# Context tiles of a cross-attention kernel: transposes moved from TensorE to VectorE blocks and DMAs inside SBUF

## The chip, the core and the metric

The kernel runs on one core of a Trainium2 chip. The metric is device time in microseconds (us). The kernel before takes 2022.62 us, the median of three runs from 2022.18 to 2022.88.

## The reference

`x` is 4096 x 512 and the context `ctx_1024` is 3202 x 512, all float32. What matters is the first half:

```
xn, cn = layernorm(x, g1, beta1), layernorm(ctx, g1, beta1)
q, k, v = heads(xn @ Wq.T + bq), heads(cn @ Wk.T + bk), heads(cn @ Wv.T + bv)   # 8 heads of 64
x1 = x + softmax(q k^T / 8) v @ W_o.T + b_o
U  = (layernorm(x1, g2, beta2) @ W_in.T + b_in) @ Bmat
s_t = silu(s_{t-1} @ A.T) + u_t          # a scan over 4096 steps
out = x1 + s @ Cmat + (mean(ctxb) @ W_prog.T + b_prog)
```

The change touches only the normalised context: how its transpose, with the 512 features on partitions, is made before the products that give `k` and `v`.

## The kernel before, in words

The program has a first stage, here called the preparation, and then the attention proper, whose instructions are put in order by a planner (`Plan`) that works with costs and due times; the scan follows interleaved with it. The change lies wholly in the preparation, whose order is written out by hand: inside `tc.manual_schedule()` every engine runs its instructions in the order of the source.

The preparation walks over 26 chunks of 128 context rows (the last has 2) in the loop `for c in range(NCH)`, line 545. Four chunks form a group (`GC = 4`). For chunk c the source order is:

1. `load_chunk(c + 7)`: SP issues the load of a raw chunk into `cx`, one of eight buffers (L509).
2. `norm_chunk(c + 3)`: VectorE takes the statistics (L245, L247), POOL makes two factors (L254 to L258), ScalarE writes the normalised chunk `xh` (L266), one of three buffers.
3. TensorE makes `pv`, eight matmuls of 128 x 512 against `wv` (L555).
4. `turn_chunk(c + 2)`: TensorE transposes `xh` in four 128 x 128 pieces into PSUM (`tp_c`, L282), and ScalarE (even chunks) or VectorE (odd chunks) copies the result into `ct` (L523). `ct` holds the turned chunks of one group, and there are two such buffers.
5. ScalarE copies `pv` to `vs`, one of three buffers (L568), and SP stores it to HBM as `vd` (L569).
6. One piece of side work (`work`, `first`): gains, biases, other small products and the loads of other weights, which ScalarE's queue issues: `raw_q`, `win`, `bm`, `bi`, `cb`, `rowb`, `modb`, `wp_t`, `a_t`, `wo`, `x0`.

After the fourth chunk of a group TensorE makes four `pk`, each eight matmuls against `wk` (L588). ScalarE writes each to `ks`, one of three buffers (L596), and SP stores each with two DMAs to `kd` (L601). PSUM has two buffers for `pv` and two for `pk`.

Two things about queues matter. SP and ScalarE each issue their DMAs in program order, and an instruction that waits holds up all that stands behind it on its engine. And the program has eight semaphores for the completion of these DMAs, `DMAHW0` to `DMAHW7`, which SP's and ScalarE's DMAs take in turn: a DMA is issued only when the one that had its semaphore before has landed.

Of the kernel before, what the change touches and what calls it, by code (L numbers as in the profile page):

```python
# [10 lines left out]
F32 = mybir.dt.float32  # L11
# [7 lines left out]

T, S2, H, NH, HD, NS = 4096, 3202, 512, 8, 64, 64  # L20
P = 128
NC = H // P
NCH = 26
CK = 128
NDC = NCH // 2
REST = S2 - (NCH - 1) * CK
GC = 4
QB = 512
NQB = T // QB
NT = QB // P  # L30
QU = QB // 2
# [20 lines left out]
def keys(c):  # L52


    return CK if c < NCH - 1 else REST
# [7 lines left out]
def key0(c):  # L63
    return c * CK
# [105 lines left out]
def xattn_ssm_kernel(  # L170
# [22 lines left out]
    nc = tc.nc  # L193
# [3 lines left out]

    kd = dram.tile([NC, NDC, P, 2 * CK], F32, name="kd")
    vd = dram.tile([NC, NDC, CK, 2, P], F32, name="vd")
    const = ctx.enter_context(tc.tile_pool(name="const", bufs=1))  # L200

    u = const.tile([P, L, NCK], F32, name="u")
    END = NCK - QU // L
    nc.gpsimd.memset(u[NS:, :, END:], 0.0)

    ident = const.tile([P, P], F32, name="ident")
    make_identity(nc, ident)
# [3 lines left out]
    nc.vector.tensor_tensor(twice, ident[:, :HD], ident[:, HD:], ALU.add)  # L211
    shifts = const.tile([P, NQB * NC], F32, name="shifts")
    kx = const.tile([P, NC, HD], F32, name="kx")
    vx = const.tile([P, H], F32, name="vx")
    nc.gpsimd.memset(vx, 0.0)
    neg_half = const.tile([P, 1], F32, name="neg_half")
    nc.gpsimd.memset(neg_half, -0.5)
    g1s = const.tile([P, NC], F32, name="g1s")
    be1s = const.tile([P, NC], F32, name="be1s")
    g2s = const.tile([P, NC], F32, name="g2s")  # L220
# [20 lines left out]
    def stats(xt, n, name, pool=None):  # L241

        pool = pool or ln
        st = pool.tile([P, nc.vector.BN_STATS_DIM], F32, tag="st", name=f"st_{name}")
        nc.vector.bn_stats(st[:n], xt[:n])  # L245
        mv = pool.tile([P, nc.vector.BN_AGGR_DIM], F32, tag="mv", name=f"mv_{name}")
        nc.vector.bn_aggr(mv[:n], st[:n])  # L247
        return mv

    def factors(mv, n, name, pool=None):  # L250

        pool = pool or ln
        ve = pool.tile([P, 1], F32, tag="ve", name=f"ve_{name}")
        nc.gpsimd.tensor_scalar(ve[:n], mv[:n, 1:2], EPS, None, ALU.add)  # L254
        rstd = pool.tile([P, 1], F32, tag="rstd", name=f"rstd_{name}")
        nc.gpsimd.tensor_tensor(rstd[:n], ve[:n], neg_half[:n], ALU.pow)
        nmr = pool.tile([P, 1], F32, tag="nmr", name=f"nmr_{name}")
        nc.gpsimd.tensor_scalar(  # L258
            nmr[:n], mv[:n, 0:1], rstd[:n], -1.0, ALU.mult, ALU.mult
        )  # L260
        return rstd, nmr
# [9 lines left out]
    def normalize(xt, n, name, later=False, pool=None):  # L271

        fs = factors(stats(xt, n, name, pool), n, name, pool)
        last = partial(scaled, xt, fs, n, name, pool)
        return last if later else last()

    def transposes(pool, tag, xh, n, name):

        name = f"tp_{name}"
        tp = pool.tile([P, NC, P], F32, tag=tag, name=name) if pool else m_tile([P, NC, P], name)  # L280
        for c in range(NC):
            nc.tensor.transpose(  # L282
                tp[:, c, :n], xh[:n, c * P : (c + 1) * P], ident[:n, :n]
            )
        return tp[:, :, :n]

    xp_ = actx.enter_context(tc.tile_pool(name="xp", bufs=2))
    xnp = actx.enter_context(tc.tile_pool(name="xnp", bufs=2))
    qp = actx.enter_context(tc.tile_pool(name="qp", bufs=6))
# [68 lines left out]
    cin = prep.enter_context(tc.tile_pool(name="cin", bufs=3))  # L358
    ctp = prep.enter_context(tc.tile_pool(name="cT", bufs=2))
# [6 lines left out]
    def fetch_w(k, queue, part=slice(0, NC)):  # L366
        queue.dma_start(raw[k][:, part], wsrc[:, part, k * H : (k + 1) * H])
# [135 lines left out]
    cxs, xhs, cts = {}, {}, {}  # L503
# [7 lines left out]

    def norm_chunk(c):
        if c < NCH:
            xhs[c] = normalize(cxs.pop(c), keys(c), f"c{c}", pool=cin)

    def turn_chunk(c):
        if c < NCH:
            g, n = c // GC, keys(c)
            if c % GC == 0:
                cts[g] = ctp.tile([P, NC, GC * CK], F32, tag="ct", name=f"ct_{g}")  # L520
            o = key0(c) - key0(g * GC)
            copy = nc.vector.tensor_copy if c % 2 else nc.scalar.copy
            copy(cts[g][:, :, o : o + n], transposes(kps, "t", xhs.pop(c), n, f"c{c}"))  # L523

    with tc.manual_schedule():
        load_chunk(0)
        nc.scalar.dma_start(g1s, g1)
        fetch_w(2, nc.scalar, slice(0, NC // 2))
        fetch_w(2, nc.sync, slice(NC // 2, NC))
        load_chunk(1)  # L530
        load_chunk(2)
        fetch_w(1, nc.scalar)
        load_chunk(3)
        for t, src in ((be1s, beta1), (bqkv, b_qkv), (g2s, g2), (be2s, beta2)):
            nc.sync.dma_start(t, src)
        for c in range(4, 7):
            load_chunk(c)
        norm_chunk(0)
        gain(2, wv)
        turn_chunk(0)  # L540
        norm_chunk(1)
        norm_chunk(2)
        work = side()
        first = shift(1)
        for c in range(NCH):
            load_chunk(c + 7)
            norm_chunk(c + 3)
            g, n = c // GC, keys(c)
            ct, o = cts[g], key0(c) - key0(g * GC)
            pv = kps.tile([P, 512], F32, tag="v", name=f"pv_{c}")  # L550
            parts = 1 if c < NCH - 1 else 2
            for i in range(NC // parts):
                for h in range(parts):
                    k = h * NC // parts + i
                    nc.tensor.matmul(  # L555
                        pv[h * HD : h * HD + n, :H],
                        ct[:, k, o : o + n],
                        wv[:, k, :],
                        start=(i == 0),
                        stop=(i == NC // parts - 1),  # L560
                        skip_group_check=True,
                    )
            if c == 0:
                turn_chunk(1)
            turn_chunk(c + 2)
            if c < NCH - 1:
                vs = cin.tile([CK, NC, P], F32, tag="vs", name=f"vs_{c}")
                nc.scalar.copy(vs, pv)  # L568
                nc.sync.dma_start(vd[:, c // 2, :, c % 2, :].rearrange("h p d -> p h d"), vs)  # L569
            else:  # L570
                second = wp.tile([n, H], F32, name="second")
                nc.scalar.copy(second, pv[HD : HD + n])
                nc.vector.tensor_tensor(vx[:n], pv[:n], second, ALU.add)
                nc.sync.dma_start(vx[HD : HD + n], vx[:n])
            if c < GC:
                if c == 1:
                    gain(1, wk)
                for _ in range((0, 1, 1, 1)[c]):
                    next(first)
            else:  # L580
                next(work, None)
            if c % GC < GC - 1 and c < NCH - 1:
                continue
            n_g = o + n
            for hp in range(NC):
                pk = kps.tile([P, 512], F32, tag="k", name=f"pk_{g}_{hp}")
                for i in range(NC):
                    nc.tensor.matmul(  # L588
                        pk[:, :n_g],
                        wk[:, i, hp * P : (hp + 1) * P],  # L590
                        ct[:, i, :n_g],
                        start=(i == 0),
                        stop=(i == NC - 1),
                    )
                ks = cin.tile([P, GC * CK], F32, tag="ks", name=f"ks_{g}_{hp}")
                nc.scalar.activation(  # L596
                    ks[:, :n_g], pk[:, :n_g], AF.Identity, bias=bias[:, NC + hp : NC + hp + 1]
                )
                for b in range(g * GC, c + 1, 2):
                    m, k = blocks(b // 2) * CK, key0(b) - key0(g * GC)  # L600
                    nc.sync.dma_start(kd[hp, b // 2, :, :m], ks[:, k : k + m])  # L601
                if g == 0:
                    nc.gpsimd.tensor_copy(kx[:, hp, REST:], ks[:, : HD - REST])
                elif c == NCH - 1:
                    nc.gpsimd.tensor_copy(kx[:, hp, :REST], ks[:, CK : CK + REST])
                for _ in range(2 if g > 1 else 1):
                    next(work, None)
        left = sum(1 for _ in work)
        assert left == 0, left
# [1074 lines left out]
    with tc.manual_schedule():  # L1684
        for g in range(AHEAD_K):
            load_k(*steps[g])
        for g in range(AHEAD):
# [4 lines left out]
                xn=2, xh=2, max=2, rd=2, o_=12,  # L1692
# [25 lines left out]
    n = nc.values_load(nbad[0:1, 0:1], min_val=0, max_val=P * (NCK + P // LT + 3 * len(units)))  # L1718
# [88 lines left out]
```

## Time and profile before

| what | before |
|---|---|
| median of the runs | 2022.62 us |
| the profiled execution's own time | 2022.73 us |
| its span, first to last instruction | 2020.9 us |
| PE (TensorE) busy | 1983.2 us, 98% |
| VectorE busy | 1170.6 us, 58% |
| ScalarE busy | 1160.3 us, 57% |
| POOL busy | 789.3 us, 39% |
| granted TensorE clock, mean | 0.995 |
| end of the preparation's last `pk` on PE | 215.1 us into the span |
| PE busy from 45 to 215 us | 169.8 of 170 us |
| VectorE busy from 45 to 215 us | 35.4 of 170 us |
| ScalarE busy from 45 to 215 us | 52.4 of 170 us |
| share of the 16 DMA engines from 45 to 215 us | 0.38 |

PE is the engine that does the matmuls, PEld its weight loads, which lie beside matmuls. Times within the span count from its first instruction. "Busy" leaves out the issuing of DMAs, so SP has no busy time in the page; its DMA instructions are seen in the timeline, in rows marked SPq. In a timeline a row gives its start, its length, the engine, the line, the operation, the tile written and the tiles read, and how many instructions were merged in it.

### The profile page before, as it was taken

Reading aid. Unit: us, or ns where it says so; the run is one execution under the profiler, and the core shown is the slowest. Engines: PE = TensorE matmul, PEld = TensorE weight load, DVE = VectorE, ACT = ScalarE, POOL = GpSimd, SP = SyncE. Lnnn points to the kernel's source line nnn. Section 1 sums busy time; section 2 is a strip of 40 time slices with the busy share of each in tenths; the row PEclk is TensorE's granted clock in tenths of the full one; section 3 lists DMA queues with packets and bytes.
Section 4 is the critical chain, followed back from the end, with each engine's and each line's share of the span. In section 5 each row is a group of like instructions: output and inputs, shape, how many; then the busy total and the mean of one; then the engine's idle time right before and its main releaser. Section 6 shows DMA issues by size and latency. Waiting matters only on the chain.

```text
span 2020.9 us, 66912 instructions
## 1 busy us (share of the span) xinstructions
PE 1983.2 (98%) x29534; PEld 1324.9 (66%) x29534; DVE 1170.6 (58%) x1481; ACT 1160.3 (57%) x1530; POOL 789.3 (39%) x631
## 2 busy tenths in 40 slices
PE   8999999999999999999999999999999999999996
PEld 4445676776677667766677667766776667766764
DVE  4321366566665666566656666566656665666575
ACT  2233566566665566556656666556655665665653
POOL 2111244235533453245523553345324552345424
PEclk9999999999999999999999999999999999999998
DMA  5632322122222322122222222232212322444475
GB/s 169 192 99 68 99 79 83 54 80 90 88 67 78 97 79 67 55 62 93 81 59 80 90 88 67 78 96 79 67 55 62 93 81 59 144 136 129 130 208 192
DMA packets 187030, 190.66 MB, mean 94 GB/s; under 512 B 20904, under 2 KB 160168, under 8 KB 186732
## 3 DMA queue, kind: packets, MB, share of 16 engines
q1 hardware_dynamic: 182184, 178.62, 29.4%
q10 hardware_dynamic: 4548, 7.67, 1.2%
q8 instruction: 235, 3.85, 0.8%
q14 instruction: 63, 0.52, 0.1%
HBM read 156.32 MB, written 29.88 MB: 92 GB/s over the span
## 4 chain that ended last, share of the span: by engine, by line
PE 78%; DVE 10%; POOL 7%; issue 3%; ACT 1%; DMA 1%; DVEq 0%; POOLq 0%; ACTq 0%
PE po L749 27%; PE s L639 27%; DVE acc L717 6%; PE pq L312 5%; PE pk L588 4%; PE pv L555 4%; POOL acc L717 4%; PE pa L933 4%; PE pd L767 1%; DVE rd L802 1%; ACT p L709 1%; PE tp_x L282 1%; DVE acc L703 1%; POOL acc L724 1%; PE sm L657 1%
## 5 line engine op out<-in xcount | busy, mean ns | idle before, releaser
L709 ACT ACTIVATE p<-s,shifts 128x1024 f32<-128x1024 f32 (+1 forms) x832 | 894.1, 1081 | 522.8 <-PE s L639 510.4
L717 DVE TENSOR_TENSOR acc<-p,acc 128x1024 f32<-128x1024 f32 (+1 forms) x515 | 620.0, 1204 | 406.9 <-POOL acc L717 310.6
L639 PE MATMUL s<-q,k 64*64 64x256 f32 x12800 | 841.4, 378 | 2.7 <-ACT p L709 1.1
L749 PE MATMUL po<-p,v 64*64 64x256 f32 x12800 | 823.2, 376 | 0.0
L717 POOL TENSOR_TENSOR acc<-p,acc 128x1024 f32<-128x1024 f32 x189 | 446.9, 2365 | 809.1 <-DVE acc L717 484.1
L639 PEld LDWEIGHTS s<-q,k 64*64 64x64 f32 x12800 | 483.9, 133 | 217.2 <-issue 21.4
L749 PEld LDWEIGHTS po<-p,v 64*64 64x64 f32 x12800 | 489.5, 133 | 189.0 <-issue 2.2
L724 POOL TENSOR_TENSOR acc<-acc 128x512 f32<-128x512 f32 x64 | 104.5, 1633 | 135.8 <-DVE acc L717 118.0
L717 DVE TENSOR_TENSOR acc<-p,p 128x1024 f32<-128x1024 f32 x64 | 84.6, 1322 | 60.1 <-ACT p L709 54.1
L312 PE MATMUL pq<-xn,wq 128*128 128x256 f32 x512 | 119.0, 385 | 0.0
L802 DVE RECIPROCAL rd<-rd 128x256 f32<-128x256 f32 (+1 forms) x65 | 112.4, 1729 | 2.2
L312 PEld LDWEIGHTS pq<-xn,wq 128*128 128x128 f32 x512 | 94.6, 190 | 23.2 <-issue 11.6
L933 PE MATMUL pa<-wo,o 128*128 128x512 f32 x240 | 107.0, 599 | 0.0
L782 DVE TENSOR_TENSOR o<-po,o 128x256 f32<-128x256 f32 x64 | 27.2, 424 | 128.4 <-ACT o L778 128.2
L555 PE MATMUL pv<-wv,ct 128*128 128x512 f32 (+1 forms) x208 | 96.4, 616 | 1.0 <-ACT ct L523 0.7
L588 PE MATMUL pk<-ct,wk 128*128 128x512 f32 (+1 forms) x224 | 88.8, 549 | 0.0
L321 ACT ACTIVATE q<-pq,bias 128x512 f32<-128x512 f32 x32 | 22.0, 687 | 108.6 <-PE pq L312 108.6
L933 PEld LDWEIGHTS pa<-wo,o 128*128 128x128 f32 x240 | 44.4, 190 | 56.0 <-issue 55.8
L703 DVE TENSOR_TENSOR acc<-x,acc 2x256 f32<-2x256 f32 x128 | 78.1, 610 | 3.0
L523 DVE COPY ct<-tp_c 128x512 f32<-128x512 f32 (+1 forms) x13 | 8.5, 651 | 105.9 <-PE tp_c L282 105.9
L555 PEld LDWEIGHTS pv<-wv,ct 128*128 128x128 f32 (+1 forms) x208 | 38.3, 193 | 44.5 <-issue 41.7
L588 PEld LDWEIGHTS pk<-ct,wk 128*128 128x128 f32 x224 | 39.2, 190 | 42.6 <-issue 42.6
(213 smaller groups left out, 1224.1 us busy)
## 6 DMA issues: line engine op xcount, KB each, us to landing
k<-kd SPq DMA_DIRECT2D x432, 128.0 KB, 2.2
v<-vd SPq DMA_DIRECT2D x432, 128.0 KB, 2.2
xr<-in_x_dram SPq DMA_DIRECT2D x32, 256.0 KB, 4.5
x1d<-xr SPq DMA_DIRECT2D x32, 256.0 KB, 2.2
x<-in_x_dram SPq DMA_DIRECT2D x28, 256.0 KB, 3.2
cx<-in_ctx_dram SPq DMA_DIRECT2D x25, 256.0 KB, 3.0
vd<-vs SPq DMA_DIRECT2D x25, 256.0 KB, 2.4
kd<-ks SPq DMA_DIRECT2D x48, 128.0 KB, 1.8
```

Of the source, the lines that this page charges most:

```text
L312: nc.tensor.matmul(pq[:, half * QU : (half + 1) * QU], wq[:, i, hp * P : (hp + 1) * P], xns[half][:, i, :], start=(i == 0), stop=(i == NC ...
L555: nc.tensor.matmul(pv[h * HD : h * HD + n, :H], ct[:, k, o : o + n], wv[:, k, :], start=(i == 0), stop=(i == NC // parts - 1), skip_group_ ...
L588: nc.tensor.matmul(pk[:, :n_g], wk[:, i, hp * P : (hp + 1) * P], ct[:, i, :n_g], start=(i == 0), stop=(i == NC - 1),)
L639: nc.tensor.matmul(s[k0 : k0 + HD, a, b, :], kts[(*w["at"][:2], c)][r, b * CK + k0 : b * CK + k0 + HD], q[r], start=True, stop=True, skip_ ...
L703: nc.vector.tensor_tensor(to[r], t[r], to[r], ALU.add)
L709: nc.scalar.activation(t[:, :, :nb, :], w["ps"][c][:, :, :nb, :], AF.Exp, bias=w["shift"])
L717: engine.tensor_tensor(w["acc"][:, :, :nb, :], t[:, :, :nb, :], before[:, :, :nb, :], ALU.add)
L724: nc.gpsimd.tensor_tensor(acc[:, :, 0, :], acc[:, :, 0, :], acc[:, :, 1, :], ALU.add)
L749: nc.tensor.matmul(w["po"][a * HD : (a + 1) * HD, k, :QU], vts[Q, hp, c][r, b, a * HD : (a + 1) * HD], t[r, a, b, :], start=(c == 0 and b ...
L782: nc.vector.tensor_tensor(o, w["po"][:, 1, :QU], o, ALU.add)
L802: nc.vector.reciprocal(w["rd"][:, part], w["rd"][:, part])
L933: nc.tensor.matmul(v["pa"], o_t[Q, c, half][:, t * P : (t + 1) * P], wo[:, c, :], start=(c == 0), stop=(c == NC - 1),)
```

## The change

Chunks 6 to 24, which are 19 of the 26, are no longer transposed by TensorE. A new function `flip_chunk(c)` lets VectorE transpose the normalised chunk within 32 x 32 blocks (`nc.vector.transpose`), which leaves every block turned but in its old place. The result goes into the chunk's own `cx` buffer, whose raw rows are no longer needed. Then `move`, called four times, issues 16 DMAs on SP, each of which carries 16 KB (32 partitions by four runs of 32 floats) from the place of a block to its right place in `ct`. The loop calls `flip_chunk(c + 4)`, so a chunk's moves stand four iterations ahead of its `pv`, and behind the load of chunk c + 7 and ahead of the store of `vd` for chunk c on SP. Chunks 0 to 5 and 25 still go through TensorE two iterations ahead. Normalisation runs ahead by five chunks in place of three from iteration 4 on; iterations 2 and 3 normalise two chunks each to get there. `ct` has two buffers as before, `cx` eight, `xh` three.

```diff
+TB = 32
+    def move(xn, of, a):
+
+        for b in range(P // TB):
+            nc.sync.dma_start(
+                xn[b * TB : (b + 1) * TB, :, a * TB : (a + 1) * TB],
+                of[a * TB : (a + 1) * TB].rearrange("p (c b k) -> p b c k", b=P // TB, k=TB)[:, b],
+            )
+
...
     def norm_chunk(c):
         if c < NCH:
-            xhs[c] = normalize(cxs.pop(c), keys(c), f"c{c}", pool=cin)
+            xhs[c] = normalize(cxs[c], keys(c), f"c{c}", pool=cin)
+
+    def group(c):
+        g = c // GC
+        if g not in cts:
+            cts[g] = ctp.tile([P, NC, GC * CK], F32, tag="ct", name=f"ct_{g}")
+        return g, key0(c) - key0(g * GC)
+
+    TURNED = 6
+
+    def flip_chunk(c):
+        if TURNED <= c < NCH - 1:
+            g, o = group(c)
+            t = cxs.pop(c)
+            nc.vector.transpose(t, xhs.pop(c))
+            for a in range(P // TB):
+                move(cts[g][:, :, o : o + CK], t, a)
 
     def turn_chunk(c):
-        if c < NCH:
-            g, n = c // GC, keys(c)
-            if c % GC == 0:
-                cts[g] = ctp.tile([P, NC, GC * CK], F32, tag="ct", name=f"ct_{g}")
-            o = key0(c) - key0(g * GC)
+        if c < TURNED or c == NCH - 1:
+            n = keys(c)
+            g, o = group(c)
             copy = nc.vector.tensor_copy if c % 2 else nc.scalar.copy
             copy(cts[g][:, :, o : o + n], transposes(kps, "t", xhs.pop(c), n, f"c{c}"))
...
         for c in range(NCH):
             load_chunk(c + 7)
-            norm_chunk(c + 3)
+            for k in (range(c + 3, c + 4), range(4, 5), range(5, 7), range(7, 9))[c] if c < 4 else [c + 5]:
+                norm_chunk(k)
+            flip_chunk(c + 4)
             g, n = c // GC, keys(c)
```

## The prediction

> **What bounds the kernel now.** I read the page's totals first, then the windows of the preparation, then the timelines of PE and of SP there.
>
> ```profile
> span 2020.9 us, 66912 instructions
> PE 1983.2 (98%) x29534; PEld 1324.9 (66%) x29534; DVE 1170.6 (58%) x1481; ACT 1160.3 (57%) x1530; POOL 789.3 (39%) x631
> ...
> q1 hardware_dynamic: 182184, 178.62, 29.4%
> q10 hardware_dynamic: 4548, 7.67, 1.2%
> ```
>
> PE is busy for 98% of the span, so an instruction taken from it is worth its length if PE stays fed. The two queue rows (packets, MB, share of 16 engines) serve below to price a small packet. The windows of groups 3 and 4 (us and count per engine, then PE clock, DMA share, GB/s):
>
> ```profile
> 113.00:143.00 30.00, 30.00 (x89) 14.48 (x88) 5.99 (x14) 11.37 (x18) 6.32 (x18) 1.00 0.35 105
> 143.00:173.00 30.00, 30.00 (x89) 14.55 (x88) 5.22 (x12) 10.89 (x17) 5.26 (x15) 1.00 0.30 88
> ```
>
> PE has no gap, VectorE (third) works 5 to 6 of 30 us, ScalarE 11. A group is 30 us long here. PE's timeline at the start of group 3:
>
> ```profile
> 112.93 3.60 PE L555 MATMUL pv<-wv,ct 128*128 128x512 f32 x8
> 116.37 0.60 PE L282 MATMUL tp_c<-ident,xh_c 128*128 128x128 f32 x4
> 116.80 0.60 PE L282 MATMUL tp_x<-ident,xh_x 128*128 128x128 f32 x4
> 117.24 3.60 PE L555 MATMUL pv<-wv,ct 128*128 128x512 f32 x8
> ```
>
> Start to start, a `pv` is 3.44 us and the four transposes of a chunk 0.43 us. SP's timeline, as the group's stores start and later in two runs of DMAs that have nothing to wait for but each other:
>
> ```profile
> 118.10 0.37 SPq L569 DMA_DIRECT2D vd<-vs  x1
> 118.57 0.46 SPq L509 DMA_DIRECT2D cx<-in_ctx_dram  x1
> ...
> 216.93 3.28 SPq L1021 DMA_DIRECT2D k<-kd  x7
> 220.25 2.82 SPq L1029 DMA_DIRECT2D v<-vd  x6
> ```
>
> One DMA alone occupies SP for 0.32 to 0.37 us, but in a row they come every 0.475 us: seven from 216.93 to 220.25. `vd` is made of four times as many runs as `k`, and its successor also starts 0.47 us after it, so the price goes by the DMA and not by its pieces. A chunk now costs SP one `cx`, one `vd` and two `kd`; between them it waits for ScalarE. That is the queue into which the change puts 16 more DMAs a chunk.
>
> **The change part by part.** The sum is made against the profiled execution: 2022.73 us, a span of 2020.9 and 1.8 around it; the median, 2022.62, is 0.1 lower.
>
> *Removed from PE.* 19 chunks x 0.43 us = 8.2 us, all on the path, since PE has no gap. Also gone are ten copies of 0.58 us on ScalarE and nine of 0.69 on VectorE, which had slack: worth nothing.
>
> *Added to VectorE.* 19 block transposes of 128x512. The trace has none. Bounds: 0.67 us (the statistics of the same tile) and 3.5 us (the reciprocal, 1729 ns for 256 elements a partition, doubled). I take 0.7, the copy of the same size. Even 3.5 a chunk is 14 us of a group's 30, beside 6: hidden by VectorE's idle time and the four-chunk lead. Without that cover it would be up to 2.8 us a chunk later for SP. The earlier normalisation moves five small instructions per chunk and adds none; in iteration 3 `xh` of chunk 8 needs the buffer of chunk 5, which PE turns in the same iteration, so ScalarE waits some 3 us there, ahead of `vs`, and PE has two `pv` buffers to bridge it: nothing. Waits for several semaphores ahead of each `pv` (51 ns each in PE's queue, L282's row) run beside the matmuls before: nothing, at worst 8 x 51 ns x 19 = 7.8 us.
>
> *Added to SP.* 19 x 16 = 304 DMAs. Price of one: between 0.365 us (alone, 0.32 and a gap of 0.045) and 0.77 (`vx<-vx`, the one DMA within SBUF, 0.728 and the gap, but of two partitions). I take 0.475, since they stand 16 in a row. Per group SP then issues 64 moves, 4 `cx`, 4 `vd`, 8 `kd`: 80 x 0.475 = 38.0 us. PE needs 30.1 - 4 x 0.43 = 28.4 us. So SP becomes the bound, 9.6 us a group. The lead of four chunks cannot soften this for long: SP's order ties it to PE. The stores of `vd` and `kd` are queued behind the moves, `ks` and `vs` have three buffers, so the fourth `ks` of a group waits until the group's first `kd` has landed, ScalarE stands, the next `vs` comes late, and PE stops at the third `pv` of the following group for want of a PSUM buffer.
>
> *Eight semaphores in turn.* A move waits for the DMA eight places earlier. 8 x 0.475 = 3.8 us against landings of 1.5 to 2.4 us: no wait among the moves. But ScalarE's loads take part, and land late (`raw_q` 6.3 us, `win` 6.1, `wo` 6.6, `x0` 6.0, `modb` 5.7). In the built program the load of chunk 10 now takes the semaphore of `raw_q`, which ScalarE issues only with the first `ks` (35.45 us), so SP stands until 35.45 + 6.3 = 41.8. `win`, `cb`, `modb`, `a_t`, `wo` and `x0` are met in the same way. Before, such waits fell into SP's idle time (0.3 us for `win`).
>
> *The sum along SP.* `xh` of chunk 6 is ready at about 29.9 us (before: 29.10 + 0.82) and its blocks soon after: moves of chunk 6 from 30.0 to 37.6, `vd` 38.1. `raw_q` until 41.8 (a wait of 3.7). `cx` and the moves of chunk 7 to 49.9, `vd` 50.4. The first `kd` lands at 50.9 + 1.8 = 52.7, frees the fourth `ks` (before at 46.7), and group 0 leaves SP at 54.2 (before 48.2). Then `win`: issued with that `ks`, landed 52.7 + 6.1 = 58.8, while SP reaches the fourth move at 56.1: 2.7 us. The other meetings in group 1 I put at 8 us together and `x0` in group 2 at 4 (bounds: 0, and one full landing of 6 us each for six of them, 36). Groups 1 to 4: 4 x 38.0 = 152. So group 4 leaves SP at 54.2 + 2.7 + 12 + 152 = 220.9; its first `kd` seven places earlier, 217.6, lands 219.4; `ks` 0.69, `xh` 0.8 and `vs` 0.58 bring the third `pv` of group 5 (chunk 22) to 221.5. Before it started at 184.33: 37.2 us later. From there PE is the bound again: the rest is 0.43 us shorter (chunk 24) and, as PE stood before it, up to 1.8 longer: the `pv` at 26.16 us followed a gap of 1.25 us, had a granted clock of 0.71 around it and took 5.38 us in place of 3.60. Earlier stops cost the same and hide behind SP. Sum: 37.2 - 0.4 + 1.8 = 38.6. The attention stage is not touched and starts that much later. 2022.7 + 38.6 = **2061 us**.
>
> *On the DMA engines.* A chunk's moves are 16 x 128 = 2048 packets of 128 B and, with 16 completions for each DMA, 2304. The queue rows give 52 ns for a mean 980 B (29.4% of 16 x 2020.9 us over 182184) and 85 ns for 1686 B, hence 12 ns for 128 B on a line: 1.7 us a chunk on each engine. SP's 9.5 us a chunk, less 0.30 x 9.5 for other traffic, leaves 6.6 us: free up to 46 ns a packet. Bounds 7 (an eighth of 52) and 52.
>
> **The rivals.**
>
> *Cheaper issues.* If moves come every 0.365 us, a group is 29.2 us of SP, hardly above PE's 28.4, and the four groups are 35 us shorter, with group 0 another 3: 2061 - 35 - 3 = 2023, plus what SP still loses when it waits for `ks`, some 5: 2028. For it speaks the median issue of `k`, 320 ns; against it, that those stand alone.
>
> *Not slower: the lead hides SP.* Then all of the 8.2 us is gained: 2014.5. It decides from an issue of 28.4 / 80 = 0.355 us downwards, and only if the loads on ScalarE's queue land before SP meets their semaphores. No issue row is below 0.364 with its gap. The Trainium skill, "DMA: Bandwidth & Descriptors", section "Issuing engines are not separate DMA queues", calls the time that a sequencer takes to initiate a DMA usually small relative to the DMA itself; by that rule 16 issues would not bind and this is the outcome. Here a 0.475 us issue stands beside a 1.8 us landing, eight of which overlap, so the row speaks against it.
>
> *Dearer moves.* At 0.77 us a group is 61.6 us: + 4 x 23.6 + 10 = 2165. Or packets beyond 46 ns: at 100 ns a chunk takes 14.4 + 2.9 us, 17.3, which is 7.8 more than SP's 9.5 over 19 chunks, 148 us, 2209. For it: no row shows a 128 B packet between partitions; against it, small packets are on the cheap side of the line above. The same page, section "Specifications", says that below 512 B the engines read, modify and write. Doubling my 12 ns would stay hidden; by it a heavier price is not excluded.
>
> **How the numbers follow.** Moves at 0.43 to 0.52 us: 0.55, the likeliest, own range 2046 to 2076 (3.5 us for each 0.01). Cheaper issues, 2026 to 2046: 0.22. Not slower: 0.09, of it 0.06 faster and 0.03 within 0.2% (4 us, about what a measurement can tell from no change). Dearer: 0.14, half of it below 2100. Slower by over 0.2%: 0.91. The range 2028 to 2100 leaves out some 0.10 below and 0.08 above.
>
> **What would show it.** After: SPq rows for the moves every 0.475 us, 7.6 us a chunk, with hardly a gap from 54 to 220; the third `pv` of each group late by some 10 us, put down to `vs`; `ks` waiting for `kd`; `tp_c` down to 28; VectorE's transpose in the table. PE clock dips after the stops. I am wrong if PE stays gapless, if the moves are spaced otherwise, if a packet is far above 46 ns, or if the preparation ends as now and the attention stage differs.

## The result, and the profile after

| | before | after |
|---|---|---|
| median | 2022.4 us (2022.12 to 2022.88, 4 runs) | 2119.3 us (2118.0 to 2121.3, 4 runs) |
| the profiled execution's own time | 2022.73 us | 2121.33 us |
| its span | 2020.9 us | 2119.5 us |
| granted TensorE clock, mean | 0.995 | 0.973 |
| end of the last `pk` of the preparation | 215.1 us | 309.3 us |
| one group on SP, end of `kd` to end of `kd` | waits for PE, 30 us | 51.2 us |

The ratio is 1.048, with a 95% interval of 1.0462 to 1.0498: slower, as forecast, but by 97 us and not by 39. It lies above the range of 2028 to 2100. In the code of after, the move is L291, the raw load L518, VectorE's transpose L537, `pv` L580, `vs` L593, the store of `vd` L594, `pk` L613, `ks` L621 and the store of `kd` L626.

The page's totals and queue rows of after (the latter: packets, MB, share of 16 engines):

```profile
span 2119.5 us, 67150 instructions
PE 1995.1 (94%) x29458; PEld 1324.6 (62%) x29458; DVE 1178.1 (56%) x1491; ACT 1154.2 (54%) x1520; POOL 789.8 (37%) x631
...
q1 hardware_dynamic: 225960, 183.62, 29.5%
...
PE 65%; DVE 10%; SPq 8%; POOL 7%; issue 4%; DMA 3%; ACT 2%; POOLq 0%; DVEq 0%; ACTq 0%
```

PE has 76 instructions fewer (19 x 4 transposes), yet its busy time has grown, since it ran at a lower clock; and in the last line, the chain that ended last, SP's queue now holds 8%. Two windows of the preparation (busy us and count of PE, PEld, VectorE, ScalarE and POOL, then PE clock, DMA share, GB/s; before: 30.00 us of PE in each 30, clock 1.00):

```profile
143.00:173.00 30.00, 14.65 (x35) 6.72 (x34) 4.43 (x9) 4.65 (x7) 3.16 (x9) 0.78 0.43 106
200.00:250.00 50.00, 31.60 (x74) 13.84 (x73) 7.08 (x14) 9.47 (x15) 5.24 (x15) 0.83 0.34 79
```

PE works half to two thirds of the time, at a granted clock of about 0.8, and VectorE and ScalarE work less than a fifth of it. The DMA engines have a share of 0.43 and 0.34. None of the columns shows who is at work. SP's timeline does, here for one group:

```profile
170.79 0.44 SPq L518 DMA_DIRECT2D cx<-in_ctx_dram  x1
171.34 10.62 SPq L291 DMA_DIRECT2D ct<-cx  x16
182.06 0.54 SPq L594 DMA_DIRECT2D vd<-vs  x1
182.64 0.50 SPq L518 DMA_DIRECT2D cx<-in_ctx_dram  x1
183.24 10.24 SPq L291 DMA_DIRECT2D ct<-cx  x16
...
206.29 10.68 SPq L291 DMA_DIRECT2D ct<-cx  x16
217.07 0.54 SPq L594 DMA_DIRECT2D vd<-vs  x1
217.70 4.23 SPq L626 DMA_DIRECT2D kd<-ks  x8
221.99 0.44 SPq L518 DMA_DIRECT2D cx<-in_ctx_dram  x1
```

Every row starts about 0.1 us or less after the last one ended: SP never rests here. Sixteen moves take 10.24 us, so that one comes every 0.644 us. From the `cx` at 170.79 to that at 221.99 a group is 51.2 us. The line's own statistics (minimum, median and maximum in ns) say the same, 599 ns and a gap of 45:

```profile
L291 SPq DMA_DIRECT2D ct<-cx x304: 585/599/1672, 30.0 to 281.8; - x152
...
DMA to landing us min/median/max: 1.8/1.9/6.7
```

How this reaches PE is read from the waits between 20 and 320 us (total, times, longest), first of ScalarE, then of PE:

```profile
ACT ks L621 <- DMA kd<-ks: 104.4, 5, 25.0
...
PE pv L580 <- ACT vs L593: 40.5, 3, 16.7
PE pq L321 <- ACT xn L314: 17.9, 1, 17.9
PE tp_x L283 <- ACT xh_x L267: 15.4, 1, 15.4
```

Five times, once a group, ScalarE stands for some 21 us before the fourth `ks`, until the group's first `kd` has landed. PE stops at what ScalarE was to make next: `vs`, or the normalised or copied tile of a piece of side work.

### The profile page after: what moved, and what is told of

The parts are those of the page before. It is cut to its first block, busy times and chain, and to the rows that moved or that the text cites. A ratio compares the mean times of both kernels' runs of the same rounds, so it can differ in the third digit from the quotient of the medians.

```text
span 2119.5 us, 67150 instructions
## 1 busy us (share of the span) xinstructions
PE 1995.1 (94%) x29458; PEld 1324.6 (62%) x29458; DVE 1178.1 (56%) x1491; ACT 1154.2 (54%) x1520; POOL 789.8 (37%) x631
## 4 chain that ended last, share of the span: by engine, by line
PE 65%; DVE 10%; SPq 8%; POOL 7%; issue 4%; DMA 3%; ACT 2%; POOLq 0%; DVEq 0%; ACTq 0%
PE po L774 25%; PE s L664 25%; SPq L291 7%; DVE acc L742 6%; PE pq L321 4%; POOL acc L742 4%; PE pa L958 3%; PE pd L792 1%; DVE rd L827 1%; ACT p L734 1%; DMA cx<-in_ctx_dram 1%; PE pk L613 1%; DVE acc L728 1%; PE pv L580 1%; PE tp_x L283 1%
## 5 line engine op out<-in xcount | busy, mean ns | idle before, releaser
L580 PE MATMUL pv<-wv,ct 128*128 128x512 f32 (+1 forms) x208 | 105.3, 668 | 41.5 <-ACT vs L593 40.5
L580 PEld LDWEIGHTS pv<-wv,ct 128*128 128x128 f32 (+1 forms) x208 | 42.7, 213 | 96.4 <-issue 50.8
L621 ACT ACTIVATE ks<-pk,bias 128x512 f32<-128x512 f32 (+1 forms) x28 | 17.8, 643 | 151.0 <-DMA kd<-ks 104.4
L613 PE MATMUL pk<-ct,wk 128*128 128x512 f32 (+1 forms) x224 | 92.9, 567 | 6.0 <-ACT ks L621 6.0
L613 PEld LDWEIGHTS pk<-ct,wk 128*128 128x128 f32 x224 | 40.8, 197 | 54.0 <-issue 46.4
```

The lines of the kernel that those rows point to most:

```text
L580: nc.tensor.matmul(pv[h * HD : h * HD + n, :H], ct[:, k, o : o + n], wv[:, k, :], start=(i == 0), stop=(i == NC // parts - 1), skip_group_ ...
L613: nc.tensor.matmul(pk[:, :n_g], wk[:, i, hp * P : (hp + 1) * P], ct[:, i, :n_g], start=(i == 0), stop=(i == NC - 1),)
```

## The experiments

The theory was that SP bounds the preparation by the number of its issues, each at a price that I had taken too low. The rivals were the packets on the DMA engines, the shortage of `ks` buffers, and a cost of the longer lead itself.

### Half of the chunks

Only the odd chunks from 7 to 23 go by VectorE and moves (`xh` has four buffers).

```diff
-        if TURNED <= c < NCH - 1:
+        if TURNED <= c < NCH - 1 and c % 2:
...
-        if c < TURNED or c == NCH - 1:
+        if c < TURNED or c == NCH - 1 or c < NCH and c % 2 == 0:
```

> Only the nine odd chunks 7 to 23 go through VectorE and moves, the even ones through TensorE; xh gets a fourth buffer. Theory, SP's issuing is the bound: a group then needs 32 x 0.644 + 16 x 0.5 = 28.6 us of SP and 30.1 - 2 x 0.43 = 29.2 us of PE, so SP no longer decides: the 9 x 0.43 = 3.9 us gained come back, less what SP still loses to stores and loads in its queue (0 to 15 us): 2018 to 2034, and the stops of PE at pv are gone from group 2 on. Rival, each move's chain (VectorE, DMA, landing) is what is late: half the moves, about half the loss: 2022 + 48 = 2070.

Measured: 2026.96 us, ratio 1.0019 (1.0009 to 1.0028). SP's timeline:

```profile
155.30 10.25 SPq L291 DMA_DIRECT2D ct<-cx  x16
```

And PE's two largest waits from 20 to 320 us:

```profile
PE tp_x L283 <- ACT xh_x L267: 2.9, 1, 2.9
PE pk L613 <- ACT ks L621: 2.3, 1, 2.3
```

A move costs the same 0.644 us, but with 32 in a group SP needs 32 x 0.644 + 16 x 0.5 = 28.6 us, about what PE needs, and 92 of the 97 us are gone. So the loss is not in proportion to the moves. It begins where SP's time passes PE's, as a bound does. The 9 x 0.43 = 3.9 us taken from PE do not show, though: the time is 4.1 us above the kernel before beside it (2022.83), of which the longer lead alone, the next run, has 2.4.

### The longer lead alone

Every chunk is transposed by TensorE, normalised five ahead as in the change (`xh` has four buffers).

```diff
-        if TURNED <= c < NCH - 1:
+        if False:
...
-        if c < TURNED or c == NCH - 1:
+        if c < NCH:
```

> Normalisation five chunks ahead as changed, but every chunk is transposed by TensorE as before; xh gets a fourth buffer. Theory: the earlier normalisation costs nothing: 2022 +- 2. Rival, the earlier normalisation delays ScalarE's vs and ks: slower by 5 us or more, PE waiting for vs.

Measured: 2025.2 us, ratio 1.0011 (1.0001 to 1.0021). That is 2.4 us above the kernel before beside it, a tenth of a per cent: a little more than the 2022 +- 2 that was expected, less than the 5 us of the rival, and PE has no wait for `vs`. The lead alone is no cause of the 97.

### Four forms of a move

In turn by chunk, the 16 DMAs have another shape and the same 16 KB. L291 is the move as it is (32 partitions, four runs of 128 B). L544 is 32 partitions with one run of 512 B. L547 is 128 partitions with 128 B. L550 is the move's shape, but read from the raw chunk in HBM. The last three bring other data than the transpose, so the output is not the reference's.

```diff
-                move(cts[g][:, :, o : o + CK], t, a)
+                if c % 4 == 0:
+                    move(ct, t, a)
...
+                        nc.sync.dma_start(ct[b * TB : (b + 1) * TB, a, :], t[a * TB : (a + 1) * TB, b * P : (b + 1) * P])
...
+                        nc.sync.dma_start(ct[:, a, b * TB : (b + 1) * TB], t[:, (a * 4 + b) * TB : (a * 4 + b + 1) * TB])
```

> Leaves out the right placing of blocks: only chunks 8, 12, 16, 20, 24 are turned rightly. Every chunk still has 16 moves of 16 KB, in four forms by c % 4: (0) as changed, 32 partitions x 4 runs of 128 B within SBUF; (1) 32 partitions x 1 run of 512 B within SBUF; (2) 128 partitions x 1 run of 128 B within SBUF; (3) 32 partitions x 4 runs of 128 B from HBM. Changed form: 0.59 us an issue, 0.64 in a row. If the third dimension of the access costs it, (1) and (2) fall to 0.43 in a row 0.475 and (3) stays; if both ends in SBUF cost it, (3) alone falls; if 32 partitions cost it, (2) alone falls; if the number of runs costs it, (1) alone falls.

Measured: one run of 2117.3 us, as the changed kernel. The lines' statistics:

```profile
L291 SPq DMA_DIRECT2D ct<-cx x80: 585/599/1082, 60.0 to 279.4; - x80
...
L544 SPq DMA_DIRECT2D ct<-cx x64: 507/589/682, 73.4 to 241.2; - x64
...
L547 SPq DMA_DIRECT2D ct<-cx x80: 464/599/1426, 30.7 to 253.0; - x80
...
L550 SPq DMA_DIRECT2D ct<-in_ctx_dram x80: 564/597/712, 43.3 to 264.0; - x80
```

All medians are 589 to 599 ns, so that none of the single causes that were named beforehand sets the price alone. Neither the number of runs (32 or 128) nor their length (128 or 512 B) nor the partitions set the price within SBUF, and the block shape keeps it when it comes from HBM. That left open why the `k` loads, in a row, cost 0.475.

### Five more forms, of 128 partitions

The chunks take five forms in turn (`f`), all of one run in each of 128 partitions. L543 is 128 B from HBM. L545 and L549 are 512 B and L547 is 1 KB, each from HBM in some chunks and within SBUF in others. There are 16, 8 or 6 DMAs a chunk, and the context tiles hold no transposed data, so the output is not the reference's.

```diff
-            for a in range(P // TB):
-                move(cts[g][:, :, o : o + CK], t, a)
+            of = t if f in (2, 4) else hbm
...
+                    nc.sync.dma_start(ct[:, i // 4, i % 4 * TB :][:, :TB], of[:, i * TB : (i + 1) * TB])
...
+                    nc.sync.dma_start(scratch[:, i * P : (i + 1) * P], of[:, i * P : (i + 1) * P])
```

> A look for the price of an issue, not for the time: the 16 moves of a chunk are replaced, in turn by chunk, by DMAs of 128 partitions of five forms, and the context tiles of chunks 6 to 24 hold no transposed data (the output is not the reference's). Form 0: 16 from HBM, 128 B a partition, 16 KB. Form 1: 8 from HBM, 512 B a partition, 64 KB. Form 2: 8 within SBUF, 512 B, 64 KB. Form 3: 2 from HBM of 1 KB a partition, 128 KB, then 4 as form 1. Form 4: 2 within SBUF of 1 KB, then 4 as form 2. If the price goes by the bytes of a partition's run (small is dear): form 0 0.64 us in a row, forms 1 to 4 0.45 to 0.48. If it goes by the source (SBUF is dear; the block form from HBM was dear for another reason): forms 2 and 4 0.64, forms 0, 1 and 3 0.475. If by something in the preparation that is common to all: all five 0.64. The time: SP has some 45 issues a group, 22 to 29 us, beside PE's 28.4: 2014 to 2030 us.

Measured: one run of 2020.2 us. SP's timeline:

```profile
117.28 7.51 SPq L543 DMA_DIRECT2D ct<-in_ctx_dram  x16
...
128.11 1.85 SPq L549 DMA_DIRECT2D ct<-in_ctx_dram  x4
...
134.37 2.54 SPq L549 DMA_DIRECT2D ct<-cx  x4
```

Same line, shape, destination and bytes: from HBM four take 1.85 us, from SBUF 2.54. With the gap that is 0.474 and 0.646 each, and 128 B from HBM cost as little as 512 B. So among DMAs of one run of 128 or 512 B in each of 128 partitions the price goes by the source: one with both ends in SBUF is the dear one. (Those of 1 KB stand only in pairs, too few to tell.) Together with the forms before: a 32-partition block is dear from either place. Why the sequencer needs longer for these is not shown by any run.

### The price alone

The changed kernel with each of its 304 moves replaced by the cheap form: 128 B in 128 partitions, from HBM. Number, order and queue of the DMAs stay, and VectorE's transpose too. The output is not the reference's, since the tiles hold raw data.

```diff
-            for a in range(P // TB):
-                move(cts[g][:, :, o : o + CK], t, a)
+            of = ctx_in[key0(c) : key0(c) + P, :]
+            for i in range(16):
+                nc.sync.dma_start(cts[g][:, i // 4, o + i % 4 * TB :][:, :TB], of[:, i * TB : (i + 1) * TB])
```

> The changed kernel, with each of its 304 moves replaced by a DMA of the same 16 KB from HBM (128 partitions x 128 B of the raw chunk), which the run before priced at 0.475 us in a row; number of DMAs, queue and order stay, and so does VectorE's transpose. The context tiles of chunks 6 to 24 then hold no transposed data, so the output is not the reference's. Theory 'of the prediction's steps only the price of a move failed': the prediction's own sum holds, a group is 38 to 39 us of SP, 2052 to 2068 us. Rival 'the way from SP's lateness to PE was sized wrong too': 2075 us or more. Rival 'the packets within SBUF are what slows the changed kernel, not SP': the issues matter little, 2014 to 2040 us.

Measured: 2068.8 us (2068.0 to 2069.6), ratio 1.0228 (1.021 to 1.0245), 0.8 us above the upper end. SP's timeline around the last full group:

```profile
177.86 4.26 SPq L627 DMA_DIRECT2D kd<-ks  x8
182.21 0.41 SPq L518 DMA_DIRECT2D cx<-in_ctx_dram  x1
182.71 7.52 SPq L540 DMA_DIRECT2D ct<-in_ctx_dram  x16
...
216.87 4.24 SPq L627 DMA_DIRECT2D kd<-ks  x8
221.20 7.53 SPq L540 DMA_DIRECT2D ct<-in_ctx_dram  x16
```

And PE's last stop:

```profile
220.82 3.78 PE L321 MATMUL pq<-xn,wq 128*128 128x256 f32 x8 [8.46 <-ACT xn L314]
```

The last full group is 39.0 us (177.86 to 216.87; the prediction had 38.0; the two before it took 41.4 and 40.3), and group 4 leaves SP at 221.1 us (the prediction had 220.9). At the price that the prediction assumed its sum along SP is met, but to the microsecond only by luck: group 0 left SP at 48.4 us (forecast 54.2), since its moves need no transpose here, group 1 took 52.0 us in place of 48.7, and the three groups behind it took 120.7 in place of 118. And 50.5 of the 97 us are the price alone (2119.3 to 2068.8), though the first moves' earlier start is in that number too. The rest of the difference to 2061 lies behind SP and is taken up below.

### Two queues

The moves with even b are issued by ScalarE, the others by SP.

```diff
-            nc.sync.dma_start(
+            (nc.sync if b % 2 else nc.scalar).dma_start(
```

> Half of the moves (b even) are issued from ScalarE's queue, half from SP's; nothing else differs from the changed kernel. Theory 'an issue is paid by the engine whose queue issues it': SP has 32 x 0.644 + 8 x 0.53 + 4 x 0.54 + 4 x 0.50 = 29.0 us a group, ScalarE 32 x 0.644 = 20.6 us more beside some 11 us of its own work in a group of PE's 28.4. ScalarE, at some 32 us, or SP is then little above PE: 2030 to 2060 us, and the rows of SP stay at 0.64 us a move. Rival 'one generator makes the descriptors for both queues, 0.644 us each': the two queues take turns, rows on each come every 1.3 us, a group stays at 51 us, 2110 to 2125 us. Rival 'the packets bind': also 2110 to 2125, but with DMA engines at a higher share in the rows of the moves.

Measured: 2079.3 us, ratio 1.0279 (1.0262 to 1.0296). ScalarE's timeline, with its queue:

```profile
151.38 5.23 ACTq L291 DMA_DIRECT2D ct<-cx  x6
156.65 0.58 ACT L593 COPY vs<-pv 128x512 f32<-128x512 f32 x1 [4.56 <-DMA ct<-cx]
157.13 0.81 ACT L267 ACTIVATE xh_c<-cx,nmr_c,rstd_c 128x512 f32<-128x512 f32 x1
157.56 6.10 ACTq L291 DMA_DIRECT2D ct<-cx  x8
163.70 0.58 ACT L593 COPY vs<-pv 128x512 f32<-128x512 f32 x1 [5.75 <-DMA ct<-cx]
```

And from its waits:

```profile
ACT vs L593 <- DMA ct<-cx: 106.7, 18, 9.8
```

The moves' statistics:

```profile
L291 SPq DMA_DIRECT2D ct<-cx x152: 585/599/846, 30.8 to 234.5; - x152
L291 ACTq DMA_DIRECT2D ct<-cx x152: 592/612/1722, 30.8 to 234.2; - x152
```

Each queue keeps its own price (medians 599 ns on SP, 612 on ScalarE) while both issue at once, which speaks against one generator for both: the issuing engine pays. But 2079 is above the 2030 to 2060 of that theory: from the first `kd` of group 2 (142.33 us) to that of group 3 (181.36) it is 39 us, in place of 32. I had added ScalarE's 20.6 us of issues to its 11 us of work, and the trace shows two more things. In its program order the moves stand in line with its waits for `pk`: the `ks`, for which it waits on PE, come some 3.4 us apart, and it issues no move meanwhile. And the eight semaphores are now taken in turn by two queues that both issue moves. Eight moves, one every 0.65 us, would take ScalarE 5.2 us; here they take 6 to 7.5. Of ScalarE's steps from move to move between 140 and 182 us, eight end within 0.06 us of a landing on the very semaphore that the move takes, and together they are 6.4 us longer than 0.644 each. No run weighs the two against each other.

### A fourth buffer for `ks`

```diff
-                ks = cin.tile([P, GC * CK], F32, tag="ks", name=f"ks_{g}_{hp}")
+                ks = cin.tile([P, GC * CK], F32, tag="ks", name=f"ks_{g}_{hp}", bufs=4)
```

> ks has four buffers in place of three, all else as in the changed kernel, so that the fourth ks of a group no longer waits for the first store of kd. Theory 'SP's issues bind': a group stays at 51 us of SP, the wait of ks for kd (25 us at a time) goes, but vs and ct then wait for the same SP: 2105 to 2120 us. Rival 'the shortage of ks buffers, not SP, holds the groups apart': four groups lose most of their 22 us, 2030 to 2050 us.

Measured: 2111.1 us, ratio 1.0434 (1.0417 to 1.0452). The wait of `ks` for `kd`, 104.4 us before, is no longer among ScalarE's large ones, and others stand in its place. From the waits of ScalarE and PE:

```profile
PE pk L613 <- ACT ks L621: 24.5, 3, 11.6
ACT vs L593 <- DMA vd<-vs: 23.6, 2, 14.6
PE pv L580 <- DMA ct<-cx: 22.1, 4, 7.1
```

PE now waits in part for the blocks themselves, in part still for ScalarE. The longest wait of the changed kernel was worth 8 us, not 104: it was mainly the place where SP's lateness arrived.

### A quarter of the issues

Chunks 8 to 23 go by VectorE and moves, but a move carries its block for all four chunks of a group: 16 DMAs of 64 KB a group in place of 64 of 16 KB (`xh` has four buffers). For that the raw chunks lie in one ring of eight, and `ct` has the chunk ahead of the feature block.

```diff
+    ring = cin.tile([P, 2 * GC, H], F32, name="cx", bufs=1)
...
-            for a in range(P // TB):
-                move(cts[g][:, :, o : o + CK], t, a)
+            if c % GC == GC - 1:
+                t = ring[:, g % 2 * GC :][:, :GC]
+                for a in range(P // TB):
+                    move(cts[g].rearrange("p j c s -> p (j c) s"), t, a)
```

> Chunks 8 to 23 go through VectorE and moves, but one move carries its block for all four chunks of a group (32 partitions x 16 runs of 128 B, 64 KB): 16 DMAs a group in place of 64, issued in the group's iteration ahead. Same bytes and packets per chunk. Theory, the price is per DMA on SP: a group is 16 x 0.65 + 16 x 0.5 = 18.4 us of SP, hidden under PE's 28.4, and 16 x 0.43 = 6.9 us are gained: 2015.5 +- 3. Rival, the packets or the runs are what costs: moves of 2.3 us each, 37 us a group beside 8, and 2100 or more.

Measured: **2016.5 us** (2015.7 to 2019.2), ratio 0.9969 (0.9958 to 0.998) to the kernel before: the fastest of all. A window of the preparation (PE, PEld, VectorE, ScalarE, POOL, clock, DMA share, GB/s):

```profile
45.00:205.00 160.00, 158.24 (x434) 72.80 (x434) 38.87 (x83) 45.32 (x70) 22.31 (x64) 1.00 0.58 148
```

The moves' statistics:

```profile
L291 SPq DMA_DIRECT2D ct<-cx x64: 585/630/2292, 60.3 to 161.8; - x64
```

SP's timeline at the end of a group:

```profile
151.72 10.74 SPq L291 DMA_DIRECT2D ct<-cx  x16
162.56 0.57 SPq L600 DMA_DIRECT2D vd<-vs  x1
```

And PE's largest wait from 20 to 320 us:

```profile
PE pv L586 <- DMA ct<-cx: 1.8, 1, 1.8
```

A move of four times the bytes costs SP 630 ns in place of 599. The packets of a chunk are as many as in the changed kernel, and the DMA share is higher, 0.58, yet PE is busy for 158.24 of 160 us. So packets are no cause; the number of issues is. (One such move comes every 0.675 us in a row, beside 0.644: the four times as many pieces cost SP a twentieth more.) The gain is 6.3 us against the kernel before beside it (2022.83), of 16 x 0.43 = 6.9 us of transposes taken from PE.

## Why the prediction was wrong in size

*What failed: the price of a move.* "I take 0.475, since they stand 16 in a row": measured 0.644. The 0.475 came from seven `k` loads, which were near in being in a row, but read HBM and have another shape (a 32-partition block cost 597 ns even from HBM). The only row within SBUF, `vx<-vx` at 0.77, stood beside it and was set aside for its two partitions; it has the same two ends. My own sensitivity, 3.5 us for 0.01, makes 59 us of the 0.169 that was missing: 2120. That this meets the measured time is partly luck, since the 3.5 charges the loads and stores as well; the 288 moves up to group 4 alone make 288 x 0.169 = 48.7 us, and the rest came from elsewhere, as below. The range had to reach the dearer of the two rows; its upper end of 2100 corresponds to 0.586 us. The step "the price goes by the DMA and not by its pieces" held within a few per cent (128 or 32 runs, 16 or 64 KB), but not the step from one DMA to another with other ends.

*What followed from it.* From SP's timeline:

```profile
267.85 4.25 SPq L626 DMA_DIRECT2D kd<-ks  x8
```

Group 4 left SP at 272.1 us in place of 220.9, 51.2 later; the moves' 48.7 are nearly all of it.

*The way to PE.* The mechanism was as written: SP full, the fourth `ks` waits for the group's first `kd`, PE stops at the third `pv`, three times (40.5 us). But twice it stopped earlier, at side work that ScalarE feeds. PE's timeline at the last stop:

```profile
271.81 3.78 PE L321 MATMUL pq<-xn,wq 128*128 128x256 f32 x8 [17.91 <-ACT xn L314]
275.38 10.60 PE L580 MATMUL pv<-wv,ct 128*128 128x512 f32 x24
```

The stop is before half of the `pq` of chunk 20's iteration; 3.57 us of it and the 3.5 us `pv` of chunk 21 were still to do. Chunk 22's `pv` starts at 278.9, 6.8 us behind SP and not 0.6: another 6.2. The run with the price alone has the same stop (`pq` from 220.82 on), and some 5 of its 8 us above 2061 are from there: its last `pk` ends at 258.95 in place of 253.7. I had taken the stop's place from the loop and forgotten the side work between two `pv`.

*The clock.* The dip at the stops is there (0.74 to 0.84 in the windows), but the 1.8 us charged to the end of the preparation is not: from chunk 22 to the last `pk` it took 30.4 us, before 30.8. So the preparation ended 51.2 + 6.2 - 1.8 = 55.6 us later than forecast, at 309.3. Another 4.4 us came behind it (2121.33 - 309.3 against 2022.73 - 215.1), of which 2.7 in the first 15 us: the first `s` starts 1.0 us later there, and over the first ten us the granted clock is 0.83 where before had 1.00. That stage was to be the same, and was not quite. Together this is the profiled execution's 60.0 above 2061.3.

*Right.* VectorE's transpose was taken at 0.7 us, and no wait is put down to it:

```profile
L537 DVE STREAM_TRANSPOSE cx<-xh_c 128x512 f32<-128x512 f32 x19 | 13.3, 702 | 57.3 <-ACT xh_c L267 44.9 <-DMA kd<-ks 12.1
```

A chunk's 0.43 us on PE is real, but only the kernel with a quarter of the issues can show it. The packets were put at 12 ns: queue q1 has 43776 more of them than before and (0.295 x 2119.5 - 0.294 x 2020.9) x 16 = 497 us more of engine time, 11 ns each. That the two agree so well is in part luck: the share of 1.2% from which the 12 came is rounded, and 1.15 or 1.25% would have given 17 or 8. So the rival of packets fails. The Trainium skill's "DMA: Bandwidth & Descriptors", section "Specifications", says that below 512 B the engines read, modify and write, which might have let one fear it; no such price is seen here. The semaphores in turn cost at most 12 to 13 us, counted as what SP's steps of over 0.8 us exceed 0.64 (1.0 in group 0, 9.8 in group 1, 1.9 in group 2; a microsecond of it is a wait for `vs`); 9 us of it are in steps that end within 0.06 us of a landing on the move's own semaphore. Forecast were 18.4, in the same groups.

*The rivals.* "Not slower" was refuted, and with it, for 64 issues a group, the rule of the Trainium skill's "DMA: Bandwidth & Descriptors", section "Issuing engines are not separate DMA queues", that the time to initiate a DMA is usually small: at 0.644 us a move it was the bound. For 16 a group it holds, at 2016.5. The Trainium skill's "Perfetto Trace Analysis", section "What 'DMA-bound' means", names the case, a solid track of the issuing sequencer, and the timeline of SP is one. It counsels large descriptors for it; here runs of 512 B cost SP as much as runs of 128 (589 and 599 ns), and it was fewer DMAs that brought the time below that of before. "Dearer moves", in its first form of a dearer issue, was nearer than the likeliest case, with its mechanism and half of its size.

## What to carry to other kernels

Price an added DMA on its queue by a row with the same two ends and the same shape, however short that row, before one that is only similar in rhythm; if the rows disagree, the range has to reach the dearer (here 0.475 and 0.77, and 0.644 came). Count issues per unit of the loop on the issuing engine, waits in program order included, and compare with the bound engine's time for the same unit: well below it they are hidden (16 moves a group: 2016.5), just below it they cost little (28.6 beside 29 us: 2027), above it every one is paid (51 beside 28: 2119). And if a mechanism is right but too dear, ask for the same bytes in fewer DMAs before giving it up.

## What was unexpected of the hardware

- In a row on SP's queue, a DMA of 128 partitions with one run each came every 0.475 us from HBM to SBUF, with 128 or 512 B a partition, and every 0.645 us from SBUF to SBUF, with 128 or 512 B. The 32-partition block of four 128 B runs was 0.64 from either.
- A move of 64 KB occupied SP for 630 ns, one of 16 KB for 599.
- SP and ScalarE issued such moves at the same time, at 599 and 612 ns each: neither made the other's issue longer. What held them up in part were the eight semaphores that they share: 6.4 us of ScalarE's queue in one group of 39.
- A DMA behind the moves was dearer too: `vd` 0.54 us and `cx` 0.50 in SP's rows of after, against 0.37 and 0.46 before; behind the cheap form from HBM `vd` was 0.38.
